# Masked attention with residual layer norms on one core: a new place for the row scalings, tails in two parts, ten key and value tiles

## The chip, the core and the metric

The kernel runs on one core of a Trainium2 chip. The metric is the time of one launch on the device in microseconds (us), as a median of several runs. Five engines work side by side, each through its own list of instructions in order: TensorE (PE; its weight loads are shown as PEld), VectorE (DVE), ScalarE (ACT), GpSimd (POOL) and SyncE (SP), which here only issues DMA transfers. Semaphores order them against each other.

## What is computed

Eight frames of 2048 rows by 256 channels go through one graph-attention layer and an outer residual norm. The mask `adj` is the same for all frames and heads (8 heads of 32 channels). All of it is float32.

```python
qkv = jnp.einsum('fnc,ck->fnk', x, w_qkv)          # q, k, v: 8 heads of 32
scores = jnp.einsum('fnhd,fmhd->fhnm', q, k) / jnp.sqrt(D)
scores = jnp.where(adj > 0, scores, -1e9)
attn = jax.nn.softmax(scores, axis=-1)
t = jnp.einsum('fhnm,fmhd->fnhd', attn, v).reshape(F, N, C)
x1 = _layernorm(x + t, ln1_g, ln1_b)
h = jax.nn.relu(jnp.einsum('fnc,cd->fnd', x1, w1) + b1)
x2 = _layernorm(x1 + jnp.einsum('fnd,dc->fnc', h, w2) + b2, ln2_g, ln2_b)
return _layernorm(x + x2)                           # no gain and bias
```

In the given inputs the gains are ones and the biases zeros.

## The kernel before

**Items.** The work is cut into 1024 items `(f, qc, g, mb)`: 8 frames, 4 chunks of 512 query rows, 2 groups of 4 heads, 16 blocks of 128 keys. A group is 16 items, a block (one query chunk of one frame) 32 items, a frame 128. Below, "position" is an item's number in its block, 0 to 31; positions 0 to 15 are group 0.

**What one item does.** `scores` (L230) makes four score matmuls on PE into two PSUM pairs of two banks each; there are three pairs in turn, so the scores of one item use a pair that the item before has used. DVE adds the mask to each pair while it moves it to a `p` tile (L233, two instructions, "the masks" below). ACT takes the exponential of the whole `p` tile (L237). `values` (L249) multiplies it with V on PE. `add_up` sums the exponentials over the blocks of keys for the softmax's denominator, in part on POOL (L271: blocks 0, 3, 6, 8, 10, 12, 14, "the sums") and in part by DMA transfers that accumulate, issued from POOL's list (L268: blocks 4, 7, 11 onto 1, and 5, 9, 13 onto 2); block 15 stays alone. The `p` pool has 12 tiles.

**The loop.** For each item t the program writes down, in this order: side work (`advance(t)`), the exponential of t+1, the scores and masks of t+2, the values of t, the sums of t. So PE's list holds for each item: scores, values, side work, and DVE's list: two masks, side work.

**Side work** is a set of generators in the list `fill`, each with an earliest item and a due item, in order of due items. A generator yields a number of items to wait, or `BANK` when it needs the one free PSUM bank; a credit in PE columns and the due item decide whether it gets it. The side work is: turning the next frame's input (`turn`), the projections to queries (`ask`) and to keys and values (`project`), and for each block

- `denominator` (L315), once per group: four terms of ones-matmuls over the summed tiles, a copy to `dT`, its transposes (L95) and on DVE a reciprocal and two checks (L326 to L328);
- `outcome`, from 6 items after the block's last: `divide` transposes the two group outputs `oT` and on DVE multiplies them with the reciprocals into a `y` tile (L353, twice); then a DMA from POOL's list adds the input rows to `y` (L339). It starts only while fewer than two tails are open (`ROOM`), and there are two `y` tiles;
- `tail`: `norm` (four row groups: statistics on DVE, L278 and L279, one row group per item; four small POOL instructions L283 to L287; two items later four normalizations on ACT, L290), `feed_forward` (transposes of `y`, first products with w1, ReLU on ACT, second products with w2, and DVE's addition of these to `y`, L483), a second `norm`, POOL's scaling by g2 and addition of be2 (L363, L365), a DMA that adds the input rows (L367), seven items, a third `norm`, and the DMA to the output (L370), issued by SP. Between the transposes and the first products POOL scales `y` by g1 and adds be1+b2 (L459, L461).

The last block ends in `finish` instead: `half_rows` does the same for two halves of the rows, after the last item, with DVE in place of some of POOL's work.

Keys and values lie in pools of 11 tiles each (8 for the frame at work, 3 for the next); `NEXT` says at which item of a frame each piece of the next frame's preparation starts.

Of the kernel before, what the change touches and what calls it, by code (L numbers as in the profile page):

```python
# [10 lines left out]
F32 = mybir.dt.float32  # L11
# [5 lines left out]
ALU = mybir.AluOpType  # L17
AX = mybir.AxisListType

P = 128  # L20
H = 8
D = 32
CH = 512
# [38 lines left out]
def fast_path(ctx, tc, cst, x, adj, out, RS):  # L62
# [5 lines left out]
    dp = ctx.enter_context(tc.tile_pool(name="dp", bufs=1, space=bass.MemoryType.DRAM))  # L68
    mkp = ctx.enter_context(tc.tile_pool(name="mkp", bufs=MB // 2 + 1))
    ld = ctx.enter_context(tc.tile_pool(name="ld", bufs=LD))  # L70
    kp = ctx.enter_context(tc.tile_pool(name="kp", bufs=3 * NCK - 1))
    qp = ctx.enter_context(tc.tile_pool(name="qp", bufs=4))
    vp = ctx.enter_context(tc.tile_pool(name="vp", bufs=3 * NCK - 1))
    pp = ctx.enter_context(tc.tile_pool(name="pp", bufs=12))
    work = ctx.enter_context(tc.tile_pool(name="work", bufs=1))
    yp = ctx.enter_context(tc.tile_pool(name="yp", bufs=2))
# [194 lines left out]
            nc.gpsimd.tensor_tensor(first, first, PT.pop(item), ALU.add)  # L271


    def norm(t, per=1):
        mv = small.tile([P, TPC, nc.vector.BN_AGGR_DIM], F32, name="mv")
        for j in range(TPC):
            st = small.tile([P, nc.vector.BN_STATS_DIM], F32, name="st")
            nc.vector.bn_stats(st, t[:, j, :])  # L278
            nc.vector.bn_aggr(mv[:, j, :], st)  # L279
            if j % per == per - 1:  # L280
                yield 1
        rs = small.tile([P, TPC], F32, name="rs")
        nc.gpsimd.tensor_scalar(rs, mv[:, :, 1], EPS, 1.0, op0=ALU.add, op1=ALU.mult)  # L283
        nc.gpsimd.tensor_tensor(rs, rs, cst["mhalf"], ALU.pow)  # L284
        nb = small.tile([P, TPC], F32, name="nb")
        nc.gpsimd.tensor_tensor(nb, mv[:, :, 0], rs, ALU.mult)
        nc.gpsimd.tensor_scalar(nb, nb, -1.0, 1.0, op0=ALU.mult, op1=ALU.mult)  # L287
        yield 2
        for j in range(TPC):
            nc.scalar.activation(t[:, j, :], t[:, j, :], AF.Identity, bias=nb[:, j:j + 1], scale=rs[:, j:j + 1])  # L290
            if j % per == per - 1:
                yield 1

    def rows(v):
        return v[:, None, :].to_broadcast([P, TPC, C])

    def denominator(f, qc, g, ready):
        grp = (f, qc, g)
        blocks = [ALONE, MOVED[0][0], POOLED[0], MOVED[1][0]]
        late = {2: ready - 1, 3: ready}  # L300
        if (f, qc, g) == items[-1][:3]:
            blocks = [POOLED[0], 11, 12, MOVED[0][0], 13, 14, MOVED[1][0], 15]
            late = {n: len(items) - k for n, k in ((2, 2), (3, 1), (4, 1), (5, 0), (6, 0), (7, 0))}
        yield BANK
        ps = bank()
        for n, block in enumerate(blocks):
            if n:
                yield MORE
            while state["now"] < late.get(n, 0):
                yield WAIT  # L310
            term = PT.pop((f, qc, g, block))
            state["credit"] -= 4 * CH
            for h in range(4):
                r = D * h
# [11 lines left out]
        nc.vector.reciprocal(rc[:, :, 4 * g:4 * g + 4], den)  # L326
        nc.vector.tensor_tensor(RS[:, 0], RS[:, 0], den, ALU.add)
        nc.vector.tensor_tensor(RS[:, 1], RS[:, 1], den, ALU.min)  # L328
        if g == 1:
            begin = items.index((f, qc, g, LAST)) + SUM + 2  # L330
            start(begin, outcome(f, qc) if (f, qc) != (F - 1, NCK - 1) else finish(f, qc), begin)

    def outcome(f, qc):
        yield ROOM
        state["tails"] += 1
        xin = x[f, qc * CH:(qc + 1) * CH, :].rearrange("(p j) c -> p j c", p=P)
        y = yp.tile([P, TPC, C], F32, name="y")
        yield from divide(f, qc, y)
        nc.gpsimd.dma_start(y, xin, accum_op=ALU.add)  # L339
        begin = items.index((f, qc, 1, LAST)) + SUM + 2  # L340
        if (f, qc) == (F - 1, NCK - 2):
            start(begin + 5, tail(f, qc, y, xin, 2), begin + 8)
        else:
            start(begin + 10, tail(f, qc, y, xin), begin + 26)

    def divide(f, qc, y):
        rc = RC.pop((f, qc))
# [6 lines left out]
                                    ps.rearrange("p (j h d) -> p j h d", h=4, d=D),  # L354
                                    rc[:, :, 4 * gg:4 * gg + 4, None].to_broadcast([P, TPC, 4, D]), ALU.mult)

    def tail(f, qc, y, xin, per=1):
        yield from norm(y, per)
        yield from feed_forward(y)
        yield 1  # L360
        z = y
        yield from norm(z, per)
        nc.gpsimd.tensor_tensor(z, z, rows(cst["g2r"]), ALU.mult)  # L363
        yield 1
        nc.gpsimd.tensor_tensor(z, z, rows(cst["be2r"]), ALU.add)  # L365
        yield 1
        nc.gpsimd.dma_start(z, xin, accum_op=ALU.add)  # L367
        yield 7
        yield from norm(z, per)
        nc.sync.dma_start(out[f, qc * CH:(qc + 1) * CH, :].rearrange("(p j) c -> p j c", p=P), z)  # L370
        state["tails"] -= 1

# [62 lines left out]
        nc.sync.dma_start(dst[:, own], z)  # L435

    def finish(f, qc):
        y = yp.tile([P, TPC, C], F32, name="y")
        xr, xb = state["rows"]
        yield from divide(f, qc, y)  # L440
        yT, hT = (work.tile([P, 2, CH], F32, name=n) for n in ("turned", "hT"))
        dst = out[f, qc * CH:(qc + 1) * CH, :].rearrange("(p j) c -> p j c", p=P)
        both = [half_rows(h, y, xr, xb, yT, hT, dst) for h in range(2)]
        while both:
            for e in list(both):
                if next(e, both) is both:
                    both.remove(e)

    def feed_forward(y):
        yield TURNED  # L450
        state["turned"] = True
        yT = work.tile([P, 2, CH], F32, name="turned")
        for a in range(2):
# [1 line left out]
            ps = bank()  # L455
            transposes(ps, [y[:, j, a * P:(a + 1) * P] for j in range(TPC)])
            nc.scalar.activation(yT[:, a, :], ps, AF.Identity, bias=cst["be1c"][:, a:a + 1], scale=cst["g1c"][:, a:a + 1])
        yield 1
        nc.gpsimd.tensor_tensor(y, y, rows(cst["g1r"]), ALU.mult)  # L459
        yield 1  # L460
        nc.gpsimd.tensor_tensor(y, y, rows(cst["be1b2r"]), ALU.add)  # L461
        hT = work.tile([P, 2, CH], F32, name="hT")
        for d in range(2):
            yield BANK
# [4 lines left out]
                columns(ps, w1s[:, a, d * P:(d + 1) * P], yT[:, a, :], start=(a == 0), stop=(a == 1))  # L469
            nc.scalar.activation(hT[:, d, :], ps, AF.Relu, bias=cst["b1s"][:, d:d + 1], scale=1.0)  # L470
        state["turned"] = False
        yield 1
        z = y
        for jj in range(0, TPC, 2):
            yield BANK
# [65 lines left out]
    def ask(f, c):  # L541
# [2 lines left out]
        give(xT)  # L544

    NEXT = {1: [(turn, 0)], 2: [(ask, 1)], 20: [(turn, 1)], 34: [(ask, 2)], 40: [(project, 0, 0)], 50: [(turn, 2)],
            60: [(project, 1, 0)], 66: [(ask, 3)], 72: [(turn, 3)], 80: [(project, 2, 0)], 98: [(ask, 0)], 100: [(project, 3, 0)],
            104: [(project, 0, 1)], 108: [(project, 1, 1)], 112: [(project, 2, 1)], 116: [(project, 3, 1)]}

    def begin():  # L550
        todo = deque((qc, c) for qc in range(NCK) for c in range(NCK))
# [319 lines left out]
```

## Time and profile before

| | |
|---|---|
| median of 3 runs | 3196.82 us (3194.78 to 3200.07) |
| the profiled execution | 3199.32 us, span 3197.5 us |
| busy: PE, DVE, POOL, ACT | 3098.8, 2737.4, 2589.4, 2438.4 us |
| mean granted PE clock | 0.987 of full |
| masks (L233) | 2048 of 1219 ns |
| exponentials (L237) | 1024 of 1911 ns |
| sums on POOL (L271) | 382 of 4866 ns |
| row statistics (L278), their aggregate (L279) | 372 of 417 ns, 372 of 182 ns |
| product with the reciprocals (L353) | 63 of 681 ns |
| POOL's scalings L459, L461, L363, L365 | 31 each of 2566, 2629, 3205, 2963 ns |
| DMA to the output (L370) | 31 of 512 KB, 5.9 us median from issue to landing |

The span is the time from the first to the last instruction of the profiled execution. A line such as "L233" is the line of the kernel printed above. A busy PE is one that has matmuls in its pipe; how fast they pass has to be read from the starts of its groups in the order of time. PE's records come twice per float32 matmul, so four matmuls are eight records.

### The profile page before, as it was taken

What the parts mean: (1) busy time and instruction counts of PE and PEld (TensorE: products, weight loads), DVE (VectorE), ACT (ScalarE), POOL (GpSimd) and SP (SyncE); (2) the same over time, 40 slices, a digit from 0 to 9 for tenths busy, and PEclk for the clock granted to TensorE, in tenths of its full rate; (3) what the DMA queues carried; (4) which work ended last, traced back from release to release, by engine and by line L of the source; (5) the groups of instructions that cost most, each with busy time, mean ns of one, the idle gap of its engine ahead of it and who ended that gap; (6) DMA issues with size and microseconds to landing.
All of it is one profiled execution on the core that took longest, in us unless ns stands there. A gap on an engine that the chain in (4) does not pass through costs nothing.

```text
span 3197.5 us, 68542 instructions
## 1 busy us (share of the span) xinstructions
PE 3098.8 (97%) x28996; PEld 980.3 (31%) x28996; DVE 2737.4 (86%) x3203; ACT 2438.4 (76%) x1941; POOL 2589.4 (81%) x1358
## 2 busy tenths in 40 slices
PE   7899999999999999999999999999999999999985
PEld 4222333233332333323333323323233233332222
DVE  4788888888889988888988988888888888889975
ACT  3677778778778777788777788778878778778764
POOL 0478888888888888789888889888888788879884
PEclk8899999999999999999999999999999999999998
DMA  9588889788879888789878889878889788878863
GB/s 322 141 193 189 181 180 194 178 190 193 182 175 210 186 191 175 175 193 208 190 172 176 190 185 221 174 169 199 180 193 207 170 191 196 178 170 167 178 142 71
DMA packets 153098, 589.49 MB, mean 184 GB/s; under 512 B 15024, under 2 KB 67760, under 8 KB 103888
## 3 DMA queue, kind: packets, MB, share of 16 engines
q0 software_dynamic: 64272, 433.75, 67.7%
q1 hardware_dynamic: 87696, 149.98, 13.4%
q8 instruction: 229, 3.75, 0.4%
q10 hardware_dynamic: 816, 1.31, 0.1%
q14 instruction: 85, 0.70, 0.1%
HBM read 146.67 MB, written 37.75 MB: 58 GB/s over the span
## 4 chain that ended last, share of the span: by engine, by line
PE 87%; DVE 5%; issue 2%; DMA 1%; POOL 1%; ACT 1%; DVEq 0%; ACTq 0%; POOLq 0%
PE s L230 32%; PE x L249 28%; PE x L54 16%; PE x L315 7%; DVE p L233 4%; PE x L95 4%; DMA p<-p 1%; DVE st L278 0%; POOL p L271 0%; DMA y<-in_x_dram 0%; DVE y L353 0%; ACT p L237 0%; PE s L54 0%; DVE mv L279 0%; ACT y L290 0%
## 5 line engine op out<-in xcount | busy, mean ns | idle before, releaser
L233 DVE TENSOR_TENSOR p<-s,mask 128x1024 f32<-128x1024 f32 x2048 | 2410.3, 1219 | 336.2 <-PE s L230 196.0
L237 ACT ACTIVATE p<-p 128x2048 f32<-128x2048 f32 x1024 | 1956.6, 1911 | 527.7 <-DVE p L233 453.7
L271 POOL TENSOR_TENSOR p<-p 128x2048 f32<-128x2048 f32 x382 | 1858.7, 4866 | 388.5 <-ACT p L237 388.2
L230 PE MATMUL s<-qT,kT 32*128 32x512 f32 x8192 | 1172.4, 642 | 40.9 <-DVE p L233 35.6
L249 PE MATMUL x<-p,v 128*32 128x512 f32 x8192 | 1092.7, 605 | 0.5 <-ACT oT L253 0.4
L230 PEld LDWEIGHTS s<-qT,kT 32*128 32x128 f32 x8192 | 320.8, 183 | 643.9 <-DVE p L233 602.5
L268 POOL DMA_DIRECT2D p<-p x382 | 408.1, 1070 | 78.4 <-ACT p L237 49.4
L249 PEld LDWEIGHTS x<-p,v 128*32 128x32 f32 x8192 | 161.4, 108 | 779.9 <-issue 289.8
L315 PE MATMUL x<-p,ones 128*32 128x512 f32 x2080 | 267.1, 592 | 0.6 <-DMA p<-p 0.5
L54 PE MATMUL x<-in,wqkv 128*32 128x512 f32 x1888 | 243.5, 592 | 0.0
L290 ACT ACTIVATE y<-y,nb,rs 128x256 f32<-128x256 f32 x372 | 218.4, 590 | 3.0 <-POOL nb L287 3.0
L278 DVE BATCH_NORM_STATS2 st<-y 128x6 f32<-128x256 f32 x372 | 155.1, 417 | 5.2 <-DMA y<-in_x_dram 5.2
L54 PE MATMUL x<-turned,w1s 128*32 128x512 f32 x992 | 122.5, 592 | 0.0
L54 PEld LDWEIGHTS x<-wqkv,in 128*32 128x32 f32 x3584 | 102.2, 110 | 63.5 <-issue 58.9
L54 PE MATMUL x<-w2s,hT 128*32 128x256 f32 x2016 | 121.1, 381 | 0.0
L54 PE MATMUL x<-wqkv,in 128*32 128x128 f32 x3584 | 117.3, 273 | 0.0
L315 PEld LDWEIGHTS x<-p,ones 128*32 128x32 f32 x2080 | 67.4, 110 | 156.8 <-issue 152.0
L54 PEld LDWEIGHTS x<-in,wqkv 128*32 128x32 f32 x1888 | 61.7, 110 | 140.9 <-issue 113.1
L284 POOL TENSOR_TENSOR rs<-rs,mhalf 128x4 f32<-128x4 f32 x93 | 96.2, 1035 | 7.7
L363 POOL TENSOR_TENSOR y<-y,g2r 128x1024 f32<-128x1024 f32 x31 | 99.3, 3205 | 1.9 <-ACT y L290 1.9
L365 POOL TENSOR_TENSOR y<-y,be2r 128x1024 f32<-128x1024 f32 x31 | 91.9, 2963 | 0.6
L54 PEld LDWEIGHTS x<-w2s,hT 128*32 128x32 f32 x2016 | 65.5, 111 | 70.5 <-issue 37.8
(116 smaller groups left out, 1342.1 us busy)
## 6 DMA issues: line engine op xcount, KB each, us to landing
p<-p POOLq DMA_DIRECT2D x382, 1024.0 KB, 9.7
in<-xd SPq DMA_DIRECT2D x87, 512.0 KB, 9.3
mask<-md SPq DMA_DIRECT2D x248, 128.0 KB, 7.9
y<-in_x_dram POOLq DMA_DIRECT2D x62, 512.0 KB, 9.5
p<-in_adj_dram SPq DMA_DIRECT2D x16, 1024.0 KB, 9.7
out_dram<-y SPq DMA_DIRECT2D x31, 512.0 KB, 5.9
in<-in_x_dram SPq DMA_DIRECT2D x29, 512.0 KB, 14.5
xd<-in SPq DMA_DIRECT2D x28, 512.0 KB, 10.7
```

The source lines that it names most:

```text
L54: nc.tensor.matmul(out[r:r + D], lhsT[:, r:r + D], rhs, start=start, stop=stop)
L95: nc.tensor.transpose(ps[:, j * P:(j + 1) * P], s, ident)
L230: nc.tensor.matmul(ps2[half][:, j, :], KT[f, mb // TPC, g][r:r + D, (mb % TPC) * P:(mb % TPC + 1) * P], QT[f, qc, g][r:r + D, :], start=Tr ...
L233: nc.vector.tensor_tensor(pt[:, 2 * half:2 * half + 2, :], ps, MK[f, qc, mb // 2][:, mb % 2, None, :].to_broadcast([P, 2, CH]), ALU.add)
L237: nc.scalar.activation(PT[item], PT[item], AF.Exp, scale=1.0 / math.sqrt(D))
L249: nc.tensor.matmul(O[grp][r:r + D, :], V[f, mb // TPC, g][:, mb % TPC, r:r + D], PT[item][:, h, :], start=(mb == 0), stop=(mb == LAST))
L268: nc.gpsimd.dma_start(PT[f, qc, g, chain[0]], PT.pop(item), accum_op=ALU.add)
L271: nc.gpsimd.tensor_tensor(first, first, PT.pop(item), ALU.add)
L278: nc.vector.bn_stats(st, t[:, j, :])
L290: nc.scalar.activation(t[:, j, :], t[:, j, :], AF.Identity, bias=nb[:, j:j + 1], scale=rs[:, j:j + 1])
L315: nc.tensor.matmul(ps[r:r + D, :], cst["ones"], term[:, h, :], start=(n == 0), stop=(n == len(blocks) - 1))
L363: nc.gpsimd.tensor_tensor(z, z, rows(cst["g2r"]), ALU.mult)
```

## The change

Five edits go together.

- `tail` is cut in two: `tail` ends after the first products, and `closing` (second products, second and third norm, output) is a new entry of `fill` with a due item of its own, 33 items after the block's outcome; the tail's own due item moves from 26 to 27.
- POOL's scalings are given a place: `calm()` yields to an item at a group's end or start, so that g1 with be1+b2, and g2 with be2, are issued between a group's last sum and the second of the next, both at once rather than an item apart. The second products wait until four items after the first pair of scalings was issued.
- `lag()` replaces the two items between a norm's POOL instructions and its normalizations by 2 to 4, by the place in the group. The denominator's last term is taken one item later.
- For the block before the last, the input rows are loaded by SP into a tile `xb`, and POOL adds them after the scaling by g2 (be2, zeros here, is left out at this place), in place of the scaling's be2 and the accumulating DMA; its tail starts 3 items later. `finish` takes its rows in a `p` tile, and after three rounds gives way to other side work between its rounds.
- The key and value pools have 10 tiles each in place of 11, and the later projections of the next frame start one place later in `NEXT`.

```diff
-    kp = ctx.enter_context(tc.tile_pool(name="kp", bufs=3 * NCK - 1))
+    kp = ctx.enter_context(tc.tile_pool(name="kp", bufs=3 * NCK - 2))
...
+    CALM = (LAST, 0, 1, 2, 3, 4)
+
+    def calm():
+        return 1 + (LAST - 1 - state["now"]) % MB if (state["now"] + 1) % MB not in CALM else 1
+
+    def lag():
+        return (4, 4, 4, 4, 2, 2, 2, 2, 2, 2, 3, 3, 3, 4, 4, 4)[state["now"] % MB]
...
-        yield 2
+        yield lag()
...
-        late = {2: ready - 1, 3: ready}
+        late = {2: ready - 1, 3: ready + 1}
...
         if (f, qc) == (F - 1, NCK - 2):
-            start(begin + 5, tail(f, qc, y, xin, 2), begin + 8)
+            xb = take([P, TPC, C], F32)
+            nc.sync.dma_start(xb, xin)
+            start(begin + 8, tail(f, qc, y, xin, begin + 11, 2, xb), begin + 11)
         else:
-            start(begin + 10, tail(f, qc, y, xin), begin + 26)
+            start(begin + 10, tail(f, qc, y, xin, begin + 33), begin + 27)
...
-    def tail(f, qc, y, xin, per=1):
+    def tail(f, qc, y, xin, due, per=1, xb=None):
         yield from norm(y, per)
-        yield from feed_forward(y)
+        second = yield from feed_forward(y, xb is not None)
+        start(state["now"] + 1, closing(f, qc, y, second, xin, per, xb), due)
+
+    def closing(f, qc, y, second, xin, per, xb):
+        yield from second
         yield 1
         z = y
         yield from norm(z, per)
-        nc.gpsimd.tensor_tensor(z, z, rows(cst["g2r"]), ALU.mult)
-        yield 1
-        nc.gpsimd.tensor_tensor(z, z, rows(cst["be2r"]), ALU.add)
-        yield 1
-        nc.gpsimd.dma_start(z, xin, accum_op=ALU.add)
-        yield 7
-        yield from norm(z, per)
+        if xb is None:
+            yield calm()
+            nc.gpsimd.tensor_tensor(z, z, rows(cst["g2r"]), ALU.mult)
+            nc.gpsimd.tensor_tensor(z, z, rows(cst["be2r"]), ALU.add)
+            yield 1
+            nc.gpsimd.dma_start(z, xin, accum_op=ALU.add)
+            yield 7
+        else:
+            nc.gpsimd.tensor_tensor(z, z, rows(cst["g2r"]), ALU.mult)
+            nc.gpsimd.tensor_tensor(z, z, xb, ALU.add)
+            yield 2
+        yield from norm(z, per if xb is None else TPC)
...
     def finish(f, qc):
-        y = yp.tile([P, TPC, C], F32, name="y")
+        y = pp.tile([P, 4, CH], F32, name="p")[:, 0:2, :].rearrange("p a (b c) -> p (a b) c", c=C)
...
+            rounds += 1
+            if rounds > 3:
+                yield 1
+
+    def feed_forward(y, soon):
...
-        yield 1
-        nc.gpsimd.tensor_tensor(y, y, rows(cst["g1r"]), ALU.mult)
-        yield 1
-        nc.gpsimd.tensor_tensor(y, y, rows(cst["be1b2r"]), ALU.add)
+        scaled = []
+
+        def scale():
+            nc.gpsimd.tensor_tensor(y, y, rows(cst["g1r"]), ALU.mult)
+            nc.gpsimd.tensor_tensor(y, y, rows(cst["be1b2r"]), ALU.add)
+            scaled.append(state["now"])
+
+        def later():
+            yield calm()
+            scale()
+
+        if soon:
+            scale()
+        else:
+            start(state["now"], later(), state["now"])
...
         state["turned"] = False
-        yield 1
+        return second_products(y, hT, scaled)
+
+    def second_products(y, hT, scaled):
+        while not scaled or state["now"] < scaled[0] + 4:
+            yield 1
         z = y
...
-            60: [(project, 1, 0)], 66: [(ask, 3)], 72: [(turn, 3)], 80: [(project, 2, 0)], 98: [(ask, 0)], 100: [(project, 3, 0)],
-            104: [(project, 0, 1)], 108: [(project, 1, 1)], 112: [(project, 2, 1)], 116: [(project, 3, 1)]}
+            60: [(project, 1, 0)], 66: [(ask, 3)], 72: [(turn, 3)], 98: [(ask, 0)], 100: [(project, 2, 0)],
+            104: [(project, 3, 0)], 108: [(project, 0, 1)], 112: [(project, 1, 1)], 116: [(project, 2, 1)], 120: [(project, 3, 1)]}
```

More of the change, by code (lines that the diff above doesn't have):

```diff
@@ L70, in fast_path @@
     ld = ctx.enter_context(tc.tile_pool(name="ld", bufs=LD))
-    kp = ctx.enter_context(tc.tile_pool(name="kp", bufs=3 * NCK - 1))
+    kp = ctx.enter_context(tc.tile_pool(name="kp", bufs=3 * NCK - 2))
     qp = ctx.enter_context(tc.tile_pool(name="qp", bufs=4))
-    vp = ctx.enter_context(tc.tile_pool(name="vp", bufs=3 * NCK - 1))
+    vp = ctx.enter_context(tc.tile_pool(name="vp", bufs=3 * NCK - 2))
     pp = ctx.enter_context(tc.tile_pool(name="pp", bufs=12))
@@ L443, in finish @@
         both = [half_rows(h, y, xr, xb, yT, hT, dst) for h in range(2)]
+        rounds = 0
         while both:
@@ L447, in finish @@
                     both.remove(e)
-    def feed_forward(y):
+            rounds += 1
+            if rounds > 3:
+                yield 1
+    def feed_forward(y, soon):
         yield TURNED
```

## The prediction, made before the changed kernel was run

> **What bounds the kernel now.** I read the share of each engine first, then the slices, the chain that ended last, and the windows of 100 us.
>
> ```profile
> PE 3098.8 (97%) x28996; PEld 980.3 (31%) x28996; DVE 2737.4 (86%) x3203; ACT 2438.4 (76%) x1941; POOL 2589.4 (81%) x1358
> PE   7899999999999999999999999999999999999985
> PE 87%; DVE 5%; issue 2%; DMA 1%; POOL 1%; ACT 1%; DVEq 0%; ACTq 0%; POOLq 0%
> L271 POOL TENSOR_TENSOR p<-p 128x2048 f32<-128x2048 f32 x382 | 1858.7, 4866 | 388.5 <-ACT p L237 388.2
> 1600.00:1700.00 100.00, 100.00 (x1044) 32.89 (x1044) 85.88 (x100) 76.67 (x61) 84.97 (x45) 1.00 0.84 183
> 3000.00:3100.00 100.00, 88.56 (x708) 24.50 (x708) 86.44 (x106) 73.73 (x57) 88.23 (x50) 0.95 0.79 165
> 3100.00:3200.00 100.00, 63.59 (x588) 21.32 (x584) 54.98 (x107) 49.28 (x56) 52.32 (x43) 0.84 0.33 73
> ```
>
> PE holds 87% of the chain and is full from slice 3 to slice 38; only the last 200 us are emptier. POOL's sums wait for exponentials (388.2 us); their row names no wait the other way, and a `p` tile comes round only after six items or more. So moving POOL's scalings can gain nothing by itself: what counts is what it does to the order on PE and DVE.
>
> On PE an item costs 2.07 us for scores and values (starts of the groups in the timeline), plus side work: .86 for four matmuls of 512 columns, .68 for four transposes of `dT` or `oT`, .59 of other rows, 1.72 for a pair of second products. Set against these costs, the scores' starts of items 64 to 928 lose 13 us in all, 1.7 per frame: .98 at two items without side work, .26 where transposes of the input follow the products of L353, .45 scattered. The first 64 items lose 33, the blocks from 928, 960 and 992 lose 4.4, 5.0 and 16.8, and 55 us lie after item 1022. All of the sum below is what changes in these losses; PE's own side work is the same before and after (935 us over all items, counted from the instruction lists).
>
> DVE is nearly full too: the mask pair is 2.36, a row group's statistics .47, a product with the reciprocals .52, an addition L483 .52, the reciprocal with its checks .24. How DVE passes its lateness on shows around the products, in DVE's timeline and in PE's:
>
> ```profile
> 1737.85 0.23 DVE L326 RECIPROCAL rc<-x 128x16 f32<-128x16 f32 x1
> ...
> 1738.09 2.35 DVE L233 TENSOR_TENSOR p<-s,mask 128x1024 f32<-128x1024 f32 x2
> 1740.36 0.68 DVE L353 TENSOR_TENSOR y<-x,rc 128x512 f32<-128x512 f32 x1
> 1740.96 2.34 DVE L233 TENSOR_TENSOR p<-s,mask 128x1024 f32<-128x1024 f32 x2
> 1743.22 0.68 DVE L353 TENSOR_TENSOR y<-x,rc 128x512 f32<-128x512 f32 x1
> ```
> ```profile
> 1736.51 1.14 PE L230 MATMUL s<-qT,kT 32*128 32x512 f32 x8
> ...
> 1739.37 1.14 PE L230 MATMUL s<-qT,kT 32*128 32x512 f32 x8
> ...
> 1742.22 1.14 PE L230 MATMUL s<-qT,kT 32*128 32x512 f32 x8
> ...
> 1745.08 1.14 PE L230 MATMUL s<-qT,kT 32*128 32x512 f32 x8
> ```
>
> PE's items here take 2.86, 2.85 and 2.86 where their matmuls cost 2.75, 2.75 and 2.66: with DVE at 2.87 per item, PE keeps DVE's step. The rule I read from this: scores n+1 start when PE is done, but not before the first half of mask n has ended (1.24 after its start, and .04); mask n starts 1.27 after its scores, or when DVE is free.
>
> **The change, by parts.**
>
> *Closing, calm and lag: a crowd on DVE.* The instruction lists show that in every block the second products now come at positions 7 and 8 (before: 4 and 5), since they wait for the scalings and g1's place is the calm of the next group. The second norm's statistics, at 6 to 9 before, now stand at 9, 10, 11 and 12: with the reciprocal at 9 and the products L353 at 10 and 11. I take the scores of position 9 as 0:
> - mask 9 is 1.27 to 3.63; statistics .47 and reciprocal .24: DVE free at 4.34. Scores 10 at 2.75, unhurt.
> - mask 10 is 4.34 to 6.70, first half done at 5.58; L353 and statistics .99: free at 7.69. Scores 11 at 5.62 where PE was ready at 5.50: .12 late.
> - mask 11 starts at 7.69, first half 8.93, free at 11.04. Scores 12 at 8.97 where PE was ready at 8.37: .60 late.
> - mask 12 starts at 11.04, first half 12.28, then only statistics. Scores 13 at 12.32, PE with input transposes ready at 11.63: .69. Scores 14: another .17.
>
> That is 1.58 per block. Where products of .86 in place of transposes stand at 13 it is 1.41, where at 12 already 1.14, and in a frame's first block, with V's projection beside them, .27. Per frame that is 4.40, and 4.85 with the scattered .45; the two empty items at position 17 are filled, so their .98 is gone. Against 1.7 this is +3.15 a frame, and for the 27 blocks of items 64 to 928 +21.2. Bounds: −7 if DVE's excess were wholly covered (.98 a frame gained), and +56 if all of it came through (2.5 per block, four statistics of .47 and .6 for late starts, times 27, less 11.5 lost before); I take the chain since the four rows above follow it to .05.
>
> *Closing: the output meets the next block.* There are two `y` tiles. The last normalization, and with it the output's DMA, now ends at position 8; the L353 of position 10 writes the same tile two items later (before, 6 to 11 items) and waits on DVE, with mask 11, all later masks, and so PE behind it. By the lists' places and the times above there are 7.3 us from issue to that wait in three blocks of four, 8.2 in the fourth. What a transfer takes:
>
> ```profile
> out_dram<-y SPq DMA_DIRECT2D x31, 512.0 KB, 5.9
> DMA to landing us min/median/max: 2.6/5.9/8.0
> xd<-in SPq DMA_DIRECT2D x28, 512.0 KB, 10.7
> ```
>
> The same transfer takes 8.0 at worst, a similar write of other rows 10.7 in the middle. Bounds: 0 (always 5.9) and 10.7 − 7.3 = 3.4 per block, +99 over 29. It is the same tile, queue and size as the first row, so I take near that end: one block in four some 1 us late, .25 per block, +7 over 27.
> The Trainium skill ("DMA: Bandwidth & Descriptors", section "Anatomy of one DMA — SWDGE (gpsimd) path") puts the fixed cost of a transfer at about 2 us, most of it the write's receipt; by that and an idle engine this term would be 0, which the rows, taken with all queues loaded, don't support.
>
> *The end.* Before, DVE waits for the accumulating DMA, and PE for DVE:
>
> ```profile
> 3081.76 0.43 DVE L278 BATCH_NORM_STATS2 st<-y 128x6 f32<-128x256 f32 x1 [5.23 <-DMA y<-in_x_dram]
> ...
> 3084.20 2.09 PE L230 MATMUL s<-qT,kT 32*128 32x512 f32 x8 [6.61 <-DVE p L233]
> 3131.60 1.14 PE L230 MATMUL s<-qT,kT 32*128 32x512 f32 x8 [1.72 <-DVE p L233]
> ```
>
> The tail's start 3 items later gives the DMA some 8 us more, so 5.23 ends. Block 992: 16.8 less 6.6 of wait and about 1.8 of slow matmuls after it (2.09 and 1.94 against 1.14 and 1.06) is 8.4, and I let 1.7 of the same DMA's wait stand: 10.1, so −6.7 (bounds −8.4 and 0). Blocks 928 and 960 get the crowd, but with their own losses already there: +1.5.
> The Trainium skill ("TensorE: Matmul & The Clock Gate", Part 1) says an idle window of about 3.4 us halves the clock; the two rows above agree (6.61 did, 1.72 didn't), so output waits of 1 to 2 us would cost no more than themselves, and only waits beyond about 3.4 us some 2 more.
>
> In `finish`, DVE's list now has the block-before-last's four statistics ahead of the second L353 (3156.18 before). They wait for ACT's copy of `dT` (ends 3154.2), then four normalizations 2.07, the scaling by g2 2.39, the addition 2.4 (both as at L363 and L365 at 3145 and 3147), and take 1.9: L353 at 3163, 7 us later, and the last output from 3188.6 to about 3196.3. But no third norm comes after it (output at 3193.33 before, 4.2 ahead of the end): the end moves to 3200.5, +3 (bounds −2 and +7).
>
> *Ten tiles, later projections, the denominator's last term*: their work fills other items; the keys' tiles are asked for later than they come free, and no PE wait names them. 0, as the lists give PE no new wait there; bounds 0 and the empties' .49 per frame, +4.
>
> **Sum**, against the profiled span 3197.5: +21.2 + 7 + 1.5 − 6.7 + 3 = +26. That execution took 3199.32, 2.5 above the median of 3196.82; forecast 3196.8 + 26 = 3223. Alone it spans 3205 (no output wait, half the crowd) to 3245 (1 us of output wait in each block). About .2%, 6.4 us, is what this kernel's runs can tell from no change.
>
> **Rivals.**
> - *The output wait decides.* For: it lies in DVE's list in every block, the write of L370 has 8.0 on its row, and a similar one 10.7. Against: 5.9 median. At 8 to 10.7 in most blocks it costs .7 to 3.4 each, 3245 to 3315.
> - *Faster: the three score pairs absorb the crowd.* Its place is positions 9 to 13: if PE can run ahead there by one pair, 1.3 us per block is covered, the crowd costs nothing, the filled empties give .98 per frame and some start and block losses (−12 with the scattered ones), the end −6.7 + 3: 3181. It decides from a slack of about 1.2 us per block on. Against: the 2.86 items above, where PE had no such slack.
> - *Nothing that counts.* PE does the same work and the gains at the end pay for a crowd of a quarter of my size without output waits: 3191 to 3203.
>
> **How the numbers follow.** Forecast .60, output wait .16, faster .13, nothing .11. Without the forecast's own tails: 3188 to 3264 leaves about .12 below and .08 above. Faster by over 6.4 us (under 3190.4) .15, within it .10 (up to 3203.2), slower .75, which holds the forecast and the output wait.
>
> **What would show it.** Right: scores at positions 10 to 13 take 2.87, 3.3, 3.3 and some 2.8 us; PE's waits there name the masks; DVE waits for the output's DMA at L353 in some blocks; the 5.23 and 6.61 waits are gone; the span ends with an output of `finish`. Wrong: items 11 and 12 at 2.75, or PE losses at other positions, or output landings over 8 us.

## The result, and the profile after

The changed kernel takes 3458.26 us (median of 4 runs, 3454.86 to 3462.24) against 3197.4 us before: a ratio of 1.0816, 95% interval 1.0798 to 1.0835. It is 261 us slower where 26 were forecast, and 194 above 3264, the upper end of the range without the forecast's own tails.

The page of the changed kernel's profile, first the busy times, the slices, the chain that ended last (by engine and by line), then the row of POOL's accumulating transfers, then two rows of transfers (KB each, us to landing):

```profile
PE 3175.4 (92%) x28996; PEld 998.1 (29%) x28996; DVE 2737.7 (79%) x3203; ACT 2439.9 (71%) x1941; POOL 2594.7 (75%) x1357
PE   7899999999999999999989999899998999999886
PE 39%; DMA 30%; DVE 14%; POOL 9%; ACT 3%; issue 3%; POOLq 0%; DVEq 0%; ACTq 0%
DMA p<-p 23%; PE s L230 15%; PE x L249 12%; DVE p L233 11%; PE x L54 8%; DMA out_dram<-y 6%; POOL p L271 4%; PE x L323 3%; ACT p L237 2%; POOL y L379 2%; POOL y L380 2%; DVE st L286 1%; PE x L95 1%; DVE y L363 1%; POOL rs L292 1%
L268 POOL DMA_DIRECT2D p<-p x382 | 371.9, 992 | 243.8 <-DMA p<-p 117.3
p<-p POOLq DMA_DIRECT2D x382, 1024.0 KB, 10.5
out_dram<-y SPq DMA_DIRECT2D x31, 512.0 KB, 9.7
```

PE held 87% of the chain before and holds 39% now; transfers hold 30%, most of it `p<-p`, the accumulating transfers, where all transfers together had 1%. No engine does more work (DVE and ACT are busy for the same time; PE's 77 us more are matmuls at a lower granted clock, 0.963 on average against 0.987: 3098.8 times 0.987/0.963 is 3176). So the kernel waits, and the chain names two sorts of transfer: the accumulation and the output. The view of waits (total us, times, longest) of the changed kernel:

```profile
POOL rs L291 <- DVE mv L287: 206.1, 39, 8.8
POOL p L268 <- DMA p<-p: 117.3, 48, 4.8
DVE p L233 <- DMA p<-p: 107.7, 37, 8.6
DVE y L363 <- DMA out_dram<-y: 74.8, 22, 5.4
PE x L323 <- DMA p<-p: 28.9, 22, 2.4
```

Before, hardly anybody waited for the accumulating transfers. The view of their line says who did, first before, then after (us, times):

```profile
  PEld x L315: 2.7, 4
  POOL p L268: 0.9, 1
  PE x L315: 0.5, 1
```
```profile
  POOL p L268: 126.4, 51
  DVE p L233: 107.7, 37
  PEld x L323: 50.1, 25
  PE x L323: 28.9, 22
```

Where this costs PE time is worked out as in the prediction: from the start of an item's scores to the start of the next, less the PE cost of what stands in the item. Summed over items 64 to 928, by position in the block, for every kernel of this study (us):

| kernel | run, median | lost | 2 to 4 | 9 to 13 | 25 to 27 |
|---|---|---|---|---|---|
| before | 3197 | 11.9 | 0 | 4 | 0 |
| changed | 3458 | 258.9 | 40 | 146 | 65 |
| e1 third y tile | 3372 | 172.8 | 38 | 56 | 67 |
| e2 closing early | 3274 | 88.3 | 79 | 2 | 2 |
| e3 lag of two | 3324 | 134.0 | 58 | 58 | 7 |
| e4 eleven tiles | 3466 | 258.4 | 29 | 156 | 59 |
| e5 g1 at once | 3229 | 37.8 | 0 | 18 | 1 |
| e6 late output | 3364 | 162.2 | 0 | 145 | 2 |
| e7 late scaling | 3293 and 3372 | 107.3 | 33 | 18 | 41 |
| e8 late rows | 3377 | 176.4 | 123 | 18 | 20 |
| e9 no pair | 3303 | 111.1 | 0 | 83 | 26 |
| e10 no pair, third y | 3275 | 86.8 | 0 | 59 | 25 |
| e11 e5, eleven tiles | 3225 | 34.8 | 0 | 18 | 1 |
| e12 e11, old end | 3221 | 34.2 | 0 | 18 | 0 |
| e13 no pair, rows later | 3425 | 228.7 | 0 | 225 | 1 |
| e14 before, projections | 3199 | 13.0 | 0 | 4 | 1 |
| e15 e14, late tail | 3201 | 13.0 | 0 | 4 | 1 |
| e16 crowd alone | 3244 | 57.9 | 0 | 53 | 2 |

(In e3 the column "2 to 4" takes in position 5, in e7 the last takes in position 28, and e7's losses are those of its run of 3293.) The changed kernel's 263 us of longer span are 247 here, 12 in the three last blocks, 4.3 after the last item, and next to nothing before item 64.

**The pair of scalings.** POOL's timeline at a group's start (start us, duration), before:

```profile
1755.23 5.33 POOL L271 TENSOR_TENSOR p<-p 128x2048 f32<-128x2048 f32 x1
1759.77 3.14 POOL L363 TENSOR_TENSOR y<-y,g2r 128x1024 f32<-128x1024 f32 x1
1762.99 2.38 POOL L365 TENSOR_TENSOR y<-y,be2r 128x1024 f32<-128x1024 f32 x1
1765.67 0.88 POOL L367 DMA_DIRECT2D y<-in_x_dram  x1 [0.30 <-POOL y L365]
1767.06 0.19 POOL L283 TENSOR_SCALAR rs<-mv 128x4 f32<-128x4 f32 x1 [0.50 <-DVE mv L279]
...
1768.88 4.58 POOL L271 TENSOR_TENSOR p<-p 128x2048 f32<-128x2048 f32 x1
1773.40 1.82 POOL L268 DMA_DIRECT2D p<-p  x2
```

and after the change, with the mask on DVE that suffers:

```profile
1779.06 4.56 POOL L271 TENSOR_TENSOR p<-p 128x2048 f32<-128x2048 f32 x1 [0.88 <-ACT p L237]
1792.37 0.20 POOL L291 TENSOR_SCALAR rs<-mv 128x4 f32<-128x4 f32 x1 [8.76 <-DVE mv L287]
...
1794.19 4.58 POOL L271 TENSOR_TENSOR p<-p 128x2048 f32<-128x2048 f32 x1
1798.72 2.39 POOL L379 TENSOR_TENSOR y<-y,g2r 128x1024 f32<-128x1024 f32 x1
1801.19 2.38 POOL L380 TENSOR_TENSOR y<-y,be2r 128x1024 f32<-128x1024 f32 x1
1803.51 0.91 POOL L268 DMA_DIRECT2D p<-p  x1
1804.13 1.20 POOL L382 DMA_DIRECT2D y<-in_x_dram  x1
...
1814.36 0.88 POOL L268 DMA_DIRECT2D p<-p  x1 [3.56 <-DMA p<-p]
```
```profile
1813.94 2.36 DVE L233 TENSOR_TENSOR p<-s,mask 128x1024 f32<-128x1024 f32 x2 [7.56 <-DMA p<-p]
```

Between a group's last sum and the next group's first there is a stretch in which POOL has nothing to add. Before, the pair stood in it, and the wait for the next statistics was down to 0.50. After, the stretch is empty (8.76 us of waiting), the pair follows the group's first sum, and the first accumulating transfer starts 4.8 us after that sum's end in place of at once. The next transfer onto the same tile has to wait for it, POOL's sums stand behind that transfer's issue, and a mask waits 7.56 us because its `p` tile is still being read. Of the 107.7 us that masks wait so, 86 stand at positions 25 and 26. At position 3 PE waits for such transfers with the denominator's products (21 of its 22 waits).

**The output.** Two accumulating transfers, the output's on SP's queue, the product L363 that writes the same `y` tile, and PE behind it:

```profile
1543.67 1.82 POOL L268 DMA_DIRECT2D p<-p  x2
...
1547.77 0.34 SPq L389 DMA_DIRECT2D out_dram<-y  x1
...
1558.58 0.69 DVE L363 TENSOR_TENSOR y<-x,rc 128x512 f32<-128x512 f32 x1 [3.61 <-DMA out_dram<-y]
...
1559.33 1.13 PE L95 MATMUL x<-ident,oT 128*128 128x128 f32 x4 [3.30 <-DVE y L363]
...
1561.00 2.09 PE L230 MATMUL s<-qT,kT 32*128 32x512 f32 x8 [0.54 <-DVE p L233]
```

DVE comes to the product at 1554.97 (1558.58 less 3.61), 7.2 us after the issue, and the transfer lands 10.8 us after it. PE stands 3.30 us and goes on at a lower clock: 2.09 for scores that take 1.14. The granted clock of this trace is 1.00 from 1540.0 to 1559.2 and 0.50 from 1559.4 to 1566.0.

### The profile page after: what moved, and what is told of

It is laid out like the page before. It is cut to its first block, busy times and chain, and to the rows that moved or that the text cites. A ratio compares the mean times of both kernels' runs of the same rounds, so it can differ in the third digit from the quotient of the medians.

```text
span 3460.5 us, 68478 instructions
## 1 busy us (share of the span) xinstructions
PE 3175.4 (92%) x28996; PEld 998.1 (29%) x28996; DVE 2737.7 (79%) x3203; ACT 2439.9 (71%) x1941; POOL 2594.7 (75%) x1357
## 4 chain that ended last, share of the span: by engine, by line
PE 39%; DMA 30%; DVE 14%; POOL 9%; ACT 3%; issue 3%; POOLq 0%; DVEq 0%; ACTq 0%
DMA p<-p 23%; PE s L230 15%; PE x L249 12%; DVE p L233 11%; PE x L54 8%; DMA out_dram<-y 6%; POOL p L271 4%; PE x L323 3%; ACT p L237 2%; POOL y L379 2%; POOL y L380 2%; DVE st L286 1%; PE x L95 1%; DVE y L363 1%; POOL rs L292 1%
## 5 line engine op out<-in xcount | busy, mean ns | idle before, releaser
L230 PE MATMUL s<-qT,kT 32*128 32x512 f32 x8192 | 1195.3, 654 | 112.4 <-DVE p L233 108.5
L249 PE MATMUL x<-p,v 128*32 128x512 f32 x8192 | 1111.0, 615 | 0.0
L268 POOL DMA_DIRECT2D p<-p x382 | 371.9, 992 | 243.8 <-DMA p<-p 117.3
L298 ACT ACTIVATE y<-y,nb,rs 128x256 f32<-128x256 f32 x372 | 219.3, 592 | 3.8 <-POOL nb L295 3.8
L291 POOL TENSOR_SCALAR rs<-mv 128x4 f32<-128x4 f32 x93 | 17.9, 193 | 210.6 <-DVE mv L287 206.1
L54 PE MATMUL x<-wqkv,in 128*32 128x128 f32 x3584 | 127.2, 292 | 17.4 <-DVE y L363 17.4
L54 PEld LDWEIGHTS x<-wqkv,in 128*32 128x32 f32 x3584 | 110.7, 119 | 72.3 <-issue 44.7
L95 PE MATMUL x<-ident,oT 128*128 128x128 f32 x252 | 51.0, 330 | 67.9 <-DVE y L363 67.9
L347 POOL DMA_DIRECT2D y<-in_x_dram x31 | 26.8, 865 | 112.5 <-DVE y L363 106.5
## 6 DMA issues: line engine op xcount, KB each, us to landing
p<-p POOLq DMA_DIRECT2D x382, 1024.0 KB, 10.5
```

Of the source, the lines that this page charges most:

```text
L54: nc.tensor.matmul(out[r:r + D], lhsT[:, r:r + D], rhs, start=start, stop=stop)
L95: nc.tensor.transpose(ps[:, j * P:(j + 1) * P], s, ident)
L230: nc.tensor.matmul(ps2[half][:, j, :], KT[f, mb // TPC, g][r:r + D, (mb % TPC) * P:(mb % TPC + 1) * P], QT[f, qc, g][r:r + D, :], start=Tr ...
L249: nc.tensor.matmul(O[grp][r:r + D, :], V[f, mb // TPC, g][:, mb % TPC, r:r + D], PT[item][:, h, :], start=(mb == 0), stop=(mb == LAST))
L268: nc.gpsimd.dma_start(PT[f, qc, g, chain[0]], PT.pop(item), accum_op=ALU.add)
```

## The experiments

Four for a first division.

**e1**, three `y` tiles:

```diff
-    yp = ctx.enter_context(tc.tile_pool(name="yp", bufs=2))
+    yp = ctx.enter_context(tc.tile_pool(name="yp", bufs=3))
```


> The changed kernel with three y tiles in place of two, so that the L353 products (L363 after the change) have no output transfer to wait for. In the changed kernel items at positions 11 to 13 lose 144 us between items 64 and 928, positions 2 to 4 lose 40, 25 to 27 lose 65, 30 loses 7. Theory: two causes side by side, the output wait (144 less a crowd on DVE of about 1.3 per block, so 105 to 110 us, about 120 with the last blocks) and a late start of POOL's accumulating transfers (the other 112). Expected: 3335 to 3355, positions 11 to 13 at 35 to 45 us, the other positions as before. Rival, one cause (all transfers are late together, and the output wait only follows from it or feeds it): the stalls at 2 to 4 and 25 to 27 move with it, 3250 or below, or it gains less than 50.

3372.28 us (ratio to before 1.0544, 1.0523 to 1.0565), 86 less than the changed kernel, and 17 above the 3335 to 3355 expected. Positions 9 to 13 fall from 146 to 56, the others stay. So the stalls at 2 to 4 and 25 to 27 don't hang on the output, and the crowd is 56 where 35 to 45 were foreseen.

**e2**, the closing early:

```diff
-            start(begin + 10, tail(f, qc, y, xin, begin + 33), begin + 27)
+            start(begin + 10, tail(f, qc, y, xin, begin + 26), begin + 26)
...
-        while not scaled or state["now"] < scaled[0] + 4:
+        while not scaled or state["now"] < scaled[0] + 1:
```


> The changed kernel with the closing's old due item (26 after the block's outcome) and no wait of four items after the scalings: second products at positions 3 and 4, second statistics at 5 to 8, g2's scaling at 15, output at 2. The scalings keep their calm places, lag, ten tiles and the end stay. Theory (late closing is the cause of all losses): 3185 to 3205, empty items filled, no losses at 2 to 4, 11 to 13 and 25 to 27. Rival (the calm places or the ten tiles cost by themselves): 3230 or more.

3274.42 us (1.0238, 1.0221 to 1.0255). All the changed kernel's losses are gone, and there is a new one of 79 at positions 2 and 3, which the theory had not seen. The waits of e2 name it:

```profile
DVE y L521 <- POOL y L485: 89.0, 22, 7.5
```

The addition of the second products waits for be1's addition on POOL. So the calm place of g1's scalings makes them late, and the wait of four items after them was its price.

**e3**, two items of lag:

```diff
-        yield lag()
+        yield 2
```


> The changed kernel with the two items of before in place of lag(): g2's scaling at position 18 and its transfer at 20 (changed: 20 and 21), output at position 4 (changed: 7 to 8), while second products (7, 8) and second statistics (9 to 12) stay. Theory: the output wait goes (105 to 120 us), the crowd of some 35 us stays at 11 to 13, and of the 112 us at other positions most goes if POOL's two scalings in front of the first accumulating transfers are the cause, since they now end before these: 3235 to 3260. Rival (the input rows' transfer beside the accumulating ones is the cause): the 112 stay, 3335 to 3355.

3324.15 us (1.0394, 1.0373 to 1.0414). The output wait is gone, the crowd stays (58), and 25 to 27 fall from 65 to 7: with the pair ahead of the group's first sum and its first accumulating transfers that stall ends. POOL's timeline in e3:

```profile
1724.29 2.40 POOL L379 TENSOR_TENSOR y<-y,g2r 128x1024 f32<-128x1024 f32 x1 [2.68 <-ACT y L298]
...
1732.25 4.57 POOL L271 TENSOR_TENSOR p<-p 128x2048 f32<-128x2048 f32 x1
1736.77 0.91 POOL L268 DMA_DIRECT2D p<-p  x1
```

The time is 64 us above the expectation, by a new loss of 58 at 3 to 5, and the waits of e3 say why:

```profile
ACT y L298 <- POOL nb L295: 82.3, 22, 5.1
```

The third norm's normalizations come on ACT before POOL has their factors, and the exponentials behind them wait too. lag() covers that in the changed kernel.

**e4**, eleven tiles and the old places in `NEXT`:

```diff
-    kp = ctx.enter_context(tc.tile_pool(name="kp", bufs=3 * NCK - 2))
+    kp = ctx.enter_context(tc.tile_pool(name="kp", bufs=3 * NCK - 1))
...
-            60: [(project, 1, 0)], 66: [(ask, 3)], 72: [(turn, 3)], 98: [(ask, 0)], 100: [(project, 2, 0)],
+            60: [(project, 1, 0)], 66: [(ask, 3)], 72: [(turn, 3)], 80: [(project, 2, 0)], 98: [(ask, 0)], 100: [(project, 3, 0)],
```


> The changed kernel with eleven key and value tiles and the old places of the projections. Theory: these cost nothing, 3450 to 3470, losses at the same positions. Rival (the later projections put the V work at position 11 and 12 of a frame's first block, where the output wait falls, and ten tiles make waits): 30 us or more faster.

3465.99 us (1.0837, 1.0815 to 1.0859), 258.4 lost against 258.9: the tiles and places cost nothing here.

The next four take e5 as a ground, in which the large losses are gone, and put one back at a time.

**e5**, e2 with g1's scalings at once and `yield 2` for lag():

```diff
-            start(state["now"], later(), state["now"])
+            scale()
```


> As e2 (closing's due item 26, no wait of four items), and also g1's scalings issued at once after the transposes (position 28) instead of in the calm, and lag() back at two items. Ten tiles, the later projections, g2's calm (which falls on position 15, the place of before) and the end stay. Theory: e2's loss of 69 + 10 us at positions 2 and 3 is the addition L521 waiting for be1's addition on POOL (89.0 us in its waits), which stands behind the sums when the scalings wait for the calm; at position 28 it is done in time: 3185 to 3205, no position above 3 us. Rival (the second products at 3 and 4 instead of 4 and 5 are too early whatever POOL does, or the ten tiles cost): 3230 or more.

3229.45 us (1.0103, 1.0086 to 1.012). e2's 79 are gone, as the theory said; but it stays 32 above before and at the edge of the rival. The rest are 18 at positions 10 to 12 and 14 at 14 to 17; the 14 are items without side work, four a frame here and two a frame before (5.9 us).

**e6**, e5 with `yield 13` in place of `yield 7` after the rows' transfer.

> e5 with six items more before the third norm, so that its statistics stand at 30, 31, 0 and 1 and the output's transfer starts where it does in the changed kernel; g2 and its transfer stay at 15, second statistics at 5 to 8. Theory: the output wait alone, 70 to 110 us over e5, all at positions 11 to 13, with landing near 9.7 us. Rival (the landing was only long because the accumulating transfers were late in the changed kernel): landing 6 or less and under 20 us over e5.

3364.36 us (1.0523, 1.0502 to 1.0544), 135 over e5, 127 of it at positions 9 to 13, and none at 2 to 4 and 25 to 27. The transfer's row of e6's page and its waits:

```profile
out_dram<-y SPq DMA_DIRECT2D x31, 512.0 KB, 9.7
```
```profile
DVE y L363 <- DMA out_dram<-y: 114.9, 21, 8.6
```

With the pair at its old place and only the output at position 8, it lands in 9.7 (e5's in 4.9): the place alone makes it long. The cost is above the 70 to 110 expected: in three blocks of four e6's products L363 stand at positions 8 and 9, two earlier than in the changed kernel, so the gap is smaller.

**e7** and **e8**, the pair and the rows' transfer at 20 and 21, and the rows' transfer alone (`yield 6` before the pair, or between pair and transfer, and `yield 4` after it):

> e5 with g2's pair of scalings at position 20 and its transfer of the input rows at 21, as in the changed kernel, and the output still early (position 1). Theory: POOL's late accumulating transfers alone, 60 to 115 us over e5, at positions 2 to 4 and 25 to 27, none at 11 to 13. Rival (they need the changed kernel's other delays): under 25 over e5.

> e5 with g2's scalings at 15 and only the transfer of the input rows at 21, beside the accumulating ones. Theory (POOL's time for the pair, 4.8 us in front of the first accumulating issues, is what makes them late): under 20 us over e5. Rival (the transfers share the DMA engines): as e7, 60 to 115.

Neither divides what it was meant to. e7's two runs took 3292.71 us at a mean granted clock of 0.980 and 3371.82 at 0.932; what made the second one slower is not known, and the trace is that of the first. This one is 63 above e5, inside the 60 to 115 of the theory, with 33 lost at position 2 and 41 at 25 to 28. But other waits stand there too: normalizations wait for POOL's factors (L298 for L295, as in e3, 34.8 us in 9 waits), and DVE waits for the rows (30.8 us in 7 waits), since four items are too few for that transfer. e8 (3377.15, 1.0563, 1.0542 to 1.0584) loses 123 at position 2, and its waits show the stall of e3 again, not a transfer:

```profile
ACT y L298 <- POOL nb L295: 128.6, 23, 6.9
```

So the changed kernel itself is taken as ground again, with one suspect less each time.

**e9**, without the pair:

```diff
-            nc.gpsimd.tensor_tensor(z, z, rows(cst["g2r"]), ALU.mult)
-            nc.gpsimd.tensor_tensor(z, z, rows(cst["be2r"]), ALU.add)
```


> The changed kernel without the two instructions on POOL that scale by g2 and add be2 (these are ones and zeros in the inputs); the transfer of the input rows after them stays at its place. Theory: before, POOL ran the pair in its idle stretch at a group's start (8.8 us of waiting for statistics stand there in the changed kernel); in the changed kernel the pair comes after the group's first sum, and its 4.8 us push the accumulating transfers and their followers, the losses at positions 2 to 4 (40 us), 25 to 27 (65) and 30 (7). Without it these go: 3335 to 3365, with 11 to 13 still at 110 to 150. Rival (the input rows' transfer, now between the accumulating ones, is the cause): they stay, 3440 or more.

3303.21 us (1.0327, 1.0308 to 1.0346), 155 less than the changed kernel, more than expected. Positions 2 to 4 are at 0, 25 to 27 at 26, and 9 to 13 fall too, to 83: the output lands in 7.4 in place of 9.7. These rows of e9 stand against 9.7, 117.3 and 107.7 us in the changed kernel:

```profile
out_dram<-y SPq DMA_DIRECT2D x31, 512.0 KB, 7.4
```
```profile
POOL p L268 <- DMA p<-p: 50.0, 28, 3.6
DVE p L233 <- DMA p<-p: 28.4, 7, 4.3
```

So 4.8 us of POOL work per block, at this place, cost 148 us between items 64 and 928. The kernel before does the same work without such a loss, so it is the place that costs.

**e10**, e9 with three `y` tiles.

> e9 with three y tiles as well. Theory (two costs that add up, and the crowd on DVE of 54 us at positions 11 to 13 as the rest): 3245 to 3275. Rival (the output wait and the late accumulation are one cause, so that one remedy does for both): no more than 25 us below e9.

3274.71 us (1.0238, 1.0219 to 1.0256), 29 below e9, at the upper edge of the theory and just past the rival's 25. The third tile is worth 86 with the late pair and 24 without (lost: 111.1 to 86.8): some 60 us of the output wait were the pair's doing.

**e11**, e5 with e4's edit, and **e12**, e11 with the old end:

> e5 with eleven key and value tiles and the old places of the projections. Theory: e5's rest over the kernel before, 16 us at position 11 of a frame's first block and some 14 at 14 to 17, comes from the later projections and shows only now that the larger waits are gone: 3195 to 3206. Rival (the closing's cut or the early second products cost it): 3220 or more.

> e11 with the old end as well: the block before the last keeps its accumulating transfer and its tail's start, finish takes a y tile and doesn't give way. Theory (forecast of the end: 992 gains some 6, finish loses 3): 2 to 5 us slower than e11. Rival (the new end gains nothing, since what it saves in block 992 comes back after the last item): within 2 us of e11 or faster.

e11 is 3224.78 us (1.0083, 1.0069 to 1.0097), e12 3220.56 (1.0069, 1.0055 to 1.0083). The theory of e11 falls: the losses stay where e5 has them, so ten tiles and the later places are not their cause. The item at position 11 of a frame's first block loses 2.7 in both; its list holds the transposes of `oT` and a whole projection to keys and values, which takes four items in the kernel before, and in e5's timeline PE waits there for the bank that L363 reads:

```profile
1649.00 1.92 PE L54 MATMUL x<-in,wqkv 128*32 128x512 f32 x16 [1.57 <-DVE y L363]
```

What shifts the projections there was not found. The new end isn't a gain either: all five runs with the old one (3219.65 to 3221.96) lie below all five of e11 (3222.74 to 3225.73), and the block from 992 loses 11.8 us with it against 15.8.

**e13**, e9 with the rows' transfer three items later (`yield 4` before it, `yield 5` after):

> e9 (g2's pair left out) with the transfer of the input rows three items later (position 24 in place of 21), behind the group's first three accumulating transfers; the output stays at 8. Theory: the 24 us that e9 still loses at positions 26 and 27 come from that transfer running beside the accumulating ones: they fall below 8, 3270 to 3290. Rival (they come from the first block's projections in front, whatever the transfers do): 20 or more stay there, 3295 to 3310.

25 to 27 fall from 26 to 1, so these were the rows' transfer among the accumulating ones. The time, 3425.42 us (1.0711, 1.0691 to 1.073), is 135 above the range expected. The edit had let the output slip by one item more, and 9 to 13 now lose 225:

```profile
  DVE y L363: 151.8, 29
```

(who waited for the output, in us and times). Nearly every block waits now, 5.2 us each, where e9 has 24.5 us in 17 waits; the output also lands later, in 9.4 us in the middle in place of 7.4.

**e14**, the new places in `NEXT` alone in the kernel before, and **e15**, also its tail's start:

```diff
-            start(begin + 5, tail(f, qc, y, xin, 2), begin + 8)
+            start(begin + 8, tail(f, qc, y, xin, 2), begin + 11)
```


> The kernel before with the changed places of the projections alone (eleven tiles). Theory (the forecast's term): the two empty items per frame at position 17 are filled, 5 to 7 us faster, 3191 to 3194. Rival (an empty item is paid back, since the same work is missing elsewhere or the projections come late for the frame's start): within 2 us of before or slower.

> e14 and, in the block before the last, the tail's start three items later and its due item 11 in place of 8, with the old transfer and the old finish. Theory (the forecast's term for the end): the 5.2 us wait of DVE for the input rows goes, 5 to 8 us faster than e14, block 992 at 8 to 11 us. Rival (the tail's later end takes it back after the last item): within 2 us of e14.

e14 is 3198.56 us (1.0004, 0.9995 to 1.0013): the empty items at position 17 stay empty. e15 is 3201.3 (1.001, 1.0001 to 1.002): the 6.7 us lost at item 1004 are gone, and 7.4 are lost at item 1012; block 992 loses 16.2 against 15.9, and 2.9 us are added after the last item. Neither part is a gain alone, and no kernel of this study beats the one before.

**e16**, e13 with three `y` tiles:

> e13 (g2's pair left out, the input rows' transfer three items later) with three y tiles, so that no product L363 waits for the output. Theory (nothing is left but the crowd, 56 us at positions 11 to 13, of which 32 in three blocks of a frame and some 25 in the first block): items 64 to 928 lose 56 to 66, 3240 to 3256. Rival (a further cost of the late closing, hidden so far): 3262 or more.

3244.49 us (1.0152, 1.0108 to 1.0196), 57.9 lost: only the crowd is left. The scores' starts at positions 10 to 13 of one block, from the timeline:

```profile
1373.40 1.14 PE L230 MATMUL s<-qT,kT 32*128 32x512 f32 x8
...
1376.20 1.14 PE L230 MATMUL s<-qT,kT 32*128 32x512 f32 x8
...
1379.59 1.14 PE L230 MATMUL s<-qT,kT 32*128 32x512 f32 x8 [0.57 <-DVE p L233]
...
1383.09 1.14 PE L230 MATMUL s<-qT,kT 32*128 32x512 f32 x8 [0.78 <-DVE p L233]
```

The items from 11 and 12 take 3.39 and 3.50 us, and PE's waits name the masks.

## Why the prediction was wrong

**The step that failed** is the one that set POOL aside: "POOL's sums wait for exponentials (388.2 us); their row names no wait the other way ... So moving POOL's scalings can gain nothing by itself: what counts is what it does to the order on PE and DVE." That nobody waited for POOL before was because of where the pair stood. I named the place the pair was to go to and didn't put it into POOL's list: it is moved past the group's first sum, and ahead of the issues of the accumulating transfers, which are a chain of three onto each of two tiles. The row quoted says what POOL waited for; it doesn't say how much room its list has at another place. A `p` tile was to come round only after six items or more, and 37 masks wait 107.7 us for one whose transfer is late. 4.8 us there cost 148 of the 247 (258.9 to 111.1, e9): about 86 at positions 2 to 4, 25 to 27 and 30, the rest through a longer output transfer. The rows' transfer that goes with it costs another 25 at 25 to 27 (e13).

**The output term was mis-sized.** The place, the tile and the gap were right: 7.3 us were worked out, 7.2 are seen. The landing was taken "near that end" of 5.9 and is 9.5 on average at position 8 (9.7 median of all). The row of `xd<-in`, a write of the same size with 10.7, which I set aside as the far bound, was the better guide. Taken at .25 per block it was 7 us; the third tile shows 86, or 24 without the late pair. The rival that gave it 3245 to 3315 had the mechanism but not the pair; its lower end doesn't follow from its own price, since 29 blocks at .7 us on the 3216 without output wait give 3236.

The Trainium skill ("TensorE: Matmul & The Clock Gate", Part 1) has an idle window of about 3.4 us halve the clock. PE's 3.30 us of wait here is followed by a granted clock of 0.50 and scores of 2.09: about the page's figure, and a little under it. So the waits at this place can cost more than themselves: items 459 and 460, the two shown, lose 6.6 us where the crowd alone takes 1.4 (e16) and DVE waited 3.6.

**The crowd on DVE was right in three blocks of four**, position by position: the scores at positions 11 to 14 were forecast .12, .60, .69 and .17 late, 1.58 in all, and are .05, .64, .84 and .13 late in the block shown for e16, 1.66 in all. In a frame's last three blocks it costs 32 us over the whole stretch (positions 9 to 13 in e10), where 28 were forecast (4.13 by 6.75 frames). In the frame's first block .27 was forecast and 3.0 (e16) to 4.0 (e10) lost on average, because PE waits there for a PSUM bank that L363 reads (2.32 us at item 523 of e10), which the recurrence left out. The whole crowd is 53 us (e16) where 30 were forecast (4.40 by 6.75).

**The end.** The forecast's −6.7 in block 992 came out as +0.7 (17.5 against 16.8). Moving the tail moved the wait: in the changed kernel DVE waits 3.51 us for the input rows at item 1007, and 3.41 for the output at 1003; e15 shows the same in the kernel before. `finish` was forecast at +3 and is +4.3; the second L353 comes 7.0 us later after the copy of `dT`, as worked out:

```profile
3421.15 0.43 DVE L286 BATCH_NORM_STATS2 st<-y 128x6 f32<-128x256 f32 x1 [4.43 <-POOL y L386]
3423.29 0.66 DVE L363 TENSOR_TENSOR p<-s,rc 128x512 f32<-128x512 f32 x1
```

**The small parts.** The empty items are filled in the changed kernel (5.9 to 0), as forecast, but by its other delays and not by `NEXT` (e14). Ten tiles and the later places cost nothing in the changed kernel (e4); e5 loses 3 us more than e11, which has the old ones.

One chain stands behind most of it. In the built order, g1's calm place puts the scalings late (e2), so second products and second norm are late, so g2's pair misses the early part of its own calm, and the output ends up two items before its tile is wanted. The delays that were written in, four items and lag(), each cover a wait that comes back when they are taken out (e2, which takes the due item back too, and e3).

## What to carry to other kernels

An engine that nobody waits for may still have no room: before a step is moved, write out the moved engine's own list around the old and the new place, and look for the idle stretch that the step stands in. Count what is queued behind the new place, transfers' issues above all, since a chain of accumulating transfers hands a delay at its head on to what stands behind it: here 4.8 us per block on POOL, for which nothing had waited, became 5.5 us per block on PE. Where a transfer must land within a few items, take its time from the busiest place in the trace and not from its own median at another place; one item less, with a landing of 9.4 us in place of 7.4, cost 142 us here (e9 to e13).

## What the runs showed of the hardware

A 512 KB write to the output took 4.9 us in the middle at positions 1 and 2 of a block (e5) and 9.0 to 9.6 on average at 8 (e1, e6, the changed kernel). In the timeline of the changed kernel it is issued 4 us after two accumulating transfers of 1 MB each, which take 10.5 in the middle themselves. The Trainium skill ("DMA: Bandwidth & Descriptors", section "Queues, rings and completion order") says that each DMA engine takes its queues in turn, packet by packet; that fits a write that is slow beside two larger transfers. So does a count over all 18 traces: issued with no accumulating transfer under way the 512 KB write took 2.8 us in the middle (121 writes, 2.6 to 4.8), with one 5.9 (192 writes, 2.6 to 10.5), with two 9.2 (245 writes, 2.6 to 12.5). But the places differ as well, and no run here takes the accumulating transfers away, so the sharing is argued and not shown.

The scaling by g2 on POOL takes 2.38 us in the changed kernel and 3.2 before: the pair is faster at the place where it does harm. No run shows why.
